# The last image's closing pass cut into three parts in a convolution kernel on one core

## The chip, the core and the metric

The kernel runs on one core of one Trainium2 chip. The metric is the device time of one execution in microseconds, the median of several runs. All engines are written by their short names: PE is TensorE (the matrix unit), DVE is VectorE, ACT is ScalarE, POOL is GpSimd, and SP is SyncE, which here only issues transfers between HBM and the on-chip memory.

## The reference

A batch of four images x of 96 channels and 128 by 128 pixels passes through two blocks. The first is a state-space block (projection, depthwise convolution, four scans, a layer norm over channels, a second projection), added to x. The second one, with which this change deals, is per image:

```python
m, v = mean and variance over channels and pixels
x1, x2 = relu_split_norm(norm(x))          # positive and negative half, each normalised
out0 = 0.5 * (nc1 * x1n + nc2 * x2n) + res_coef * x
k, q, val = conv3x3(x1, aw1), conv3x3(x2, aw2), conv3x3(x1, aw3)
W = softmax(patches(k) @ patches(q).T)      # a 3x3 kernel for every pair of channels
o = conv3x3(val, W)                         # "own": each image has its own weights W
c2 = conv3x3(x2, w_conv2)                   # "second map"
y = w_full[:, 0] @ norm(o) + w_full[:, 1] @ (norm(c2) * x1) + b_full + out0 + x
```

The exact scaling factors do not matter here. What matters: the output of an image needs a product with `norm(o)`, and the statistics of `o` are known only when the last row of its own convolution is done. The product with `norm(c2) * x1` needs the statistics of c2, and those are known as soon as the maps are done, before the own convolution begins. The thresholds (`x > thr`), which give x1 and the residual, need the normalised image alone.

## The kernel before

**Two streams.** The program is written as Python generators that yield a cost. `co_run(left, light, pace)` lets a heavy stream (left) emit its instructions and lets a light one follow in proportion to the yielded costs. A scheduler then lays out each engine's order; each engine runs its own order strictly, and waits on semaphores where data come from elsewhere. For the images b = 1 to 3 left is `attention(img, at)`. The light stream holds the next image's normalisation and split, and then the closing pass of the image before, `imgs[b - 1].close(psr, "right")`. Whatever of the light stream is left when image b begins is emitted ahead of it (`drain(light)`).

**The attention of an image** goes over 11 chunks of 12 rows (the last one of 8) and has two phases:

1. The maps. For each chunk there are four products (`products`, L1470 and L1485): a convolution with 128 outputs and one with 64 for the two halves x1 and x2. Each convolution is done as six products with transformed weights. ACT copies the sums out of PSUM (L1541), and DVE puts them together (`outputs`, L1555 to L1563). Between them PE does the patch products (L1746, L1636). POOL copies the values (L1974) and makes their transformed planes. After the last chunk `taps.weights()` makes the softmax and the transformed weights, which are stacked as `wa`.
2. The own convolution with `wa`, one product per chunk. DVE takes statistics of each chunk (L2034), and SP stores it to `od` in HBM (L2037).

Inputs are loaded by SP two chunks ahead: `ya` (L1879) and `yc` (L1887). `own`, `oc`, the rings of patch rows and the stacks of weights lie in pools of the left side.

**The closing pass** is `attn_output`. It first makes the statistics: of o (`so`, `ro`) by way of `combine` (L186 to L197), of c2 by way of L2170 to L2187. From these come the two 96 by 96 weights `w1` (L2191) and `w2` (L2193) and a constant per channel `lb` (L2197). Then it goes over 16 strips of 8 rows (1024 pixels). For each it loads `o`, `c2` and `xx` (L2203, SP, 384 KB each, one strip ahead, two buffers), makes x1 (ACT L2213, DVE L2214), scales c2 (DVE L2215) and makes the residual e (ACT L2219, DVE L2220 and L2221). For each half of 512 pixels two matmuls add up in one PSUM bank (L2225 with `o`, L2226 with `c2`). DVE adds `lb` and e, and for the images 1 to 3, whose pixels lie in another order, does that in four pieces of 128 (L2237). For image 0 it is one piece (L2228). SP stores the strip (L2239).

The closing passes of the images 0 to 2 run beside the attention of a later image. The last image has none after it:

```python
    drain(light)
    drain(imgs[NB - 1].close(psr, "right"))
```

Of the kernel before, what the change touches and what calls it, by code (L numbers as in the profile page):

```python
# [9 lines left out]
F32 = mybir.dt.float32  # L10
BF16 = mybir.dt.bfloat16
AF = mybir.ActivationFunctionType
ALU = mybir.AluOpType
# [4 lines left out]
C = 96  # L18
# [39 lines left out]
HS = 8  # L58

# [9 lines left out]
def kernel(  # L69
# [1779 lines left out]
    class Attention:  # L1849
# [3 lines left out]
        def __init__(self, ps, p1, p2):  # L1853
            self.ps, self.p1, self.p2 = ps, p1, p2
            self.later = Later()
            chunks = strips_of(AR // 2)
            self.chunks = [(c[0][0], sum(r for _, r in c)) for c in chunks]
            self.todo = [(0, 2, c) for c in self.chunks]
            for b in range(1, NB):
                self.todo += [(b, m, c) for c in self.chunks for m in (0, 1)]  # L1860
                self.todo += [(b, 2, c) for c in self.chunks]
            self.raw, self.cols, self.c = {}, {}, 0
# [62 lines left out]
    def attention(img, at):  # L1925


        ps, p1, p2, later, chunks = at.ps, at.p1, at.p2, at.later, at.chunks
# [5 lines left out]
        if not img.mapped:  # L1934
            taps = PairTaps(ps, later, p1)
# [4 lines left out]
            def value_out(r0, r):  # L1940

                def f():
                    hr = r // 2
                    for i, a in enumerate((0, hr)):

                        def then(pl, a=a):
                            store_planes(nc.sync, img.vp[0:64], r0 + a, hr, pl[0:64])
                            store_planes(nc.sync, img.vp[64:96], r0 + a, hr, pl[96:128])

                        later(planes_of(  # L1950
                            later, p2, own[:, a * PP :], hr, then, AR // 2, bufs=1, p=128
                        ), 3 * i)

                return f

            for s, (r0, r) in enumerate(chunks):
                hr = r // 2
                for m in (0, 1):
# [32 lines left out]
                    if m:  # L1991
                        oc = p2.tile([128, AR // 2 * W], F32, name="oc", bufs=1)
# [31 lines left out]
            ws = product_stack(p1, taps.wt, "wa", nc.scalar)  # L2024
        else:
            ws = product_stack(p1, img.watd, "wa", nc.scalar)
        yield 3.0
        for i, (r0, r) in enumerate(chunks):
            t, fill, load = at.strip()
            oc = own[0:C, : AR * W]  # L2030

            def out(oc=oc, r0=r0, r=r):
# [4 lines left out]
                nc.sync.dma_start(img.od[:, r0 * W : (r0 + r) * W], oc[:, : r * W])  # L2037
# [110 lines left out]

    def attn_output(img, ps, side):
        keep = img.keep  # L2150
        up, low, thr, scale, shift = (keep[n] for n in ("up", "low", "thr", "scale", "shift"))
        ob = out[img.b].rearrange("c h w -> c (h w)")
        with (
# [3 lines left out]
            so, _ = combine(ps, img.ost.rearrange("p c s -> p (c s)"), mean96, "so")  # L2157
            ro = col("ro")
            rsqrt(ro, so[:, 1:2])


            n = NSTRIP
            mva, mvb = (p1.tile([128, 2], F32, name=f"mv_{i}") for i in "ab")
            for mv, st, p, e, k in (
                (mva, img.c2a, 96, 128, 4 * n - 1 if img.mapped else 3 * n - 1),
                (mvb, img.c2b, 0, 64, 2 * n - (not img.mapped)),
                (mvb, img.c2b, 64, 128, 2 * n - 1),
            ):
                v = st[p:e, :k].rearrange("p c s -> p (c s)")
                nc.vector.bn_aggr(mv[p:e], v)  # L2170
            halves = ((mva[96:128], m96[96:128]), (mvb, mrows[img.mapped]))

            def over(n):
                pt = bank(ps)[:, 0:n]
                for i, (mv, mat) in enumerate(halves):
                    nc.tensor.matmul(
                        pt, lhsT=mat, rhs=mv[:, 0:n], start=(i == 0), stop=(i == 1)
                    )
                return pt

            s2 = p1.tile([128, 2], F32, name="s2")
            nc.vector.tensor_copy(s2, over(2))
            for mv, p in ((mva, 96), (mvb, 0)):
                d = mv[p:128, 0:1]
                nc.vector.tensor_sub(d, d, s2[p:128, 0:1])
                nc.vector.tensor_mul(d, d, d)
            nc.vector.tensor_add(s2[:, 1:2], s2[:, 1:2], over(1))  # L2187
            r2 = col("r2")
            rsqrt(r2, s2[0:C, 1:2])
            w1 = p1.tile([C, C], F32, name="w1")  # L2190
            nc.vector.tensor_scalar(w1, wful[:, 0], ro, None, ALU.mult)  # L2191
            w2 = p1.tile([C, C], F32, name="w2")
            nc.vector.tensor_scalar(w2, wful[:, 1], r2, None, ALU.mult)  # L2193
            pt = bank(ps)[:C, 0:1]
            nc.tensor.matmul(pt, lhsT=w1, rhs=so[:, 0:1], start=True, stop=True)
            lb = col("lb")
            nc.vector.tensor_sub(lb, low[:, 1:2], pt)  # L2197

            def loads(t):
                got = []  # L2200
                for name, src in (("o", img.od), ("c2", img.c2d), ("xx", img.xnew)):
# [6 lines left out]
            for t in range(NS):  # L2208
# [4 lines left out]
                nc.scalar.activation(x1, xx, AF.Identity, scale=scale[:, 0:1], bias=shift[:, 0:1])  # L2213
                nc.vector.scalar_tensor_tensor(x1, xx, thr, x1, ALU.is_gt, ALU.mult)  # L2214
# [4 lines left out]
                nc.scalar.activation(e, xx, AF.Identity, scale=up[:, 0:1], bias=up[:, 1:2])  # L2219
                nc.vector.scalar_tensor_tensor(e, xx, thr, e, ALU.is_gt, ALU.mult)  # L2220
                nc.vector.scalar_tensor_tensor(e, xx, low[:, 0:1], e, ALU.mult, ALU.add)  # L2221
                for h in range(2):
# [4 lines left out]
                    if img.mapped:  # L2227
                        nc.vector.scalar_tensor_tensor(x1[:, sl], pf, lb, e[:, sl], ALU.add, ALU.add)  # L2228
                    else:
                        for a in range(0, CH, W):  # L2230
                            px, pe, po = (
                                v[:, a : a + W].rearrange("p (j t) -> p j t", j=TW)
                                if i < 2
                                else v[:, a : a + W].rearrange("p (t j) -> p j t", j=TW)
                                for i, v in enumerate((pf, e[:, sl], x1[:, sl]))
                            )
                            nc.vector.scalar_tensor_tensor(po, px, lb, pe, ALU.add, ALU.add)  # L2237
                    yield 2.6
                nc.sync.dma_start(ob[:, bass.ts(t, SN)], x1)  # L2239

    class Image:


        def __init__(self, b):
# [9 lines left out]
            self.finished = False  # L2254
            self.watd = None if b else dram.tile([C, 3, NP, C], F32, name="watd", bufs=1)
# [114 lines left out]
    for i, rows in enumerate((H // 2, H // 2 + 1)):  # L2370
# [4 lines left out]
    wp = ctx.enter_context(tc.tile_pool(name="wpairs", bufs=1, side="left"))  # L2375
    pairs = []
    at = Attention(
        psl,
        ctx.enter_context(tc.tile_pool(name="d1", bufs=1, side="left")),
        ctx.enter_context(tc.tile_pool(name="d2", bufs=2, side="left")),  # L2380
    )
    at.begin()
    pairs.extend(product_stack(wp, wd, f"wd{i}") for i, wd in enumerate(four))
    for b in range(NB):
        after = []
        if b:
# [3 lines left out]
            if b + 1 < NB:  # L2390
                imgs[b + 1] = Image(b + 1)
                after.append(imgs[b + 1].norm(yms[(b + 1) // 2][(b + 1) % 2], psr, "right"))
                after.append(imgs[b + 1].split(psr, "right", lambda i, second: second))
            after.append(imgs[b - 1].close(psr, "right"))
        light = chain(light, *after)
# [4 lines left out]
    drain(imgs[NB - 1].close(psr, "right"))  # L2400
# [75 lines left out]
```

## Time and profile before

| what | value |
|---|---|
| median of three runs | 6673.67 us (6661.18 to 6675.5) |
| the profiled execution's own time | 6664.87 us |
| its span, first to last instruction | 6663.1 us |
| PE, DVE, ACT, POOL busy | 81%, 73%, 57%, 52% of the span |
| maps of the last image, where no light stream runs beside them | 6060 to 6400 us |
| own convolution of the last image | 6407 to 6513 us |
| closing pass of the last image alone | 6513 to 6663 us |

The busy share of an engine is an average over stages with different limits, so the stages are to be read one by one. The profiled execution took 1.8 us more than its span, and it lies 8.8 us (0.13%) under the median of the runs. Sums are made against the profiled execution; a predicted median then carries the same difference.

### The profile page before, as it was taken

How to read it: one execution, taken by the hardware profiler on the slowest of the kernel's cores; microseconds unless marked ns; L12 is line 12 of the kernel's file. 1: busy time of each engine (PE TensorE's matmuls, PEld its weight loads, DVE VectorE, ACT ScalarE, POOL GpSimd, SP SyncE). 2: the span in 40 equal slices, each digit the busy share in tenths (PEclk: the TensorE clock that was granted, in tenths of full speed). 3: DMA queues.
4: the chain of work that ended last, by engine and by line, in shares of the span. 5: the costliest groups of instructions: out<-in, count | busy, mean ns of one | idle time of the engine just before them, and what ended most of it. 6: DMA issues, size and time to landing. Idle time of an engine off the chain costs nothing. (4 is left out here: it accounts for less than half of the span.)

```text
span 6663.1 us, 76540 instructions
## 1 busy us (share of the span) xinstructions
PE 5393.7 (81%) x23256; PEld 2343.1 (35%) x23256; DVE 4885.0 (73%) x7737; ACT 3810.5 (57%) x4751; POOL 3437.4 (52%) x2683
## 2 busy tenths in 40 slices
PE   5889978988887626989985579877889777878996
PEld 2333323322221103434433243444333454335642
DVE  3247778988997568979756884588865788887557
ACT  1257768777776576767534554565444664535552
POOL 2236658878786436969622363465124574023410
PEclk9999989988997758999997788988879887989987
DMA  7766777866765666765676766556765555865454
GB/s 166 173 156 180 198 212 199 225 180 171 221 186 162 186 175 208 203 194 175 196 189 175 205 167 165 157 148 163 200 182 159 145 159 153 227 164 145 103 149 143
DMA packets 882102, 1176.27 MB, mean 177 GB/s; under 512 B 215230, under 2 KB 740102, under 8 KB 869212
## 3 DMA queue, kind: packets, MB, share of 16 engines
q1 hardware_dynamic: 858076, 1116.43, 61.9%
q0 software_dynamic: 16208, 38.42, 2.1%
q10 hardware_dynamic: 7408, 16.53, 0.8%
q8 instruction: 187, 3.06, 0.2%
q14 instruction: 223, 1.83, 0.1%
HBM read 766.61 MB, written 334.57 MB: 165 GB/s over the span
## 5 line engine op out<-in xcount | busy, mean ns | idle before, releaser
L621 PE MATMUL bank<-y,wp 128*128 128x512 f32 (+3 forms) x3584 | 1315.3, 623 | 84.3 <-DMA y<-y 34.0
L854 POOL TENSOR_TENSOR y<-y,dl 128x1024 f32<-128x1024 f32 x384 | 1051.3, 2738 | 267.8 <-DVE dl L846 237.1
L821 POOL TENSOR_TENSOR dl<-dl,u 128x1024 f32<-128x1024 f32 x384 | 1007.5, 2624 | 228.0 <-ACT dA L797 116.3
L842 DVE TENSOR_TENSOR_SCAN dA<-dA,pBC 128x512 f32<-128x512 f32 x768 | 981.7, 1278 | 30.7
L1470 PE MATMUL two<-ya,wd 128*64 128x192 f32 (+3 forms) x2376 | 590.5, 426 | 189.5 <-ACT odd L1541 106.6
L735 PE MATMUL pBC<-xr,wbc 60*128 60x512 bf16 (+1 forms) x1536 | 457.1, 402 | 333.8 <-DVE dA L842 260.4
L846 DVE TENSOR_TENSOR dl<-dA,pBC 128x512 f32<-128x512 f32 x768 | 528.8, 689 | 268.2 <-PE pBC L735 195.2
L621 PEld LDWEIGHTS bank<-y,wp 128*128 128x128 f32 (+3 forms) x3584 | 458.3, 169 | 753.5 <-issue 655.5
L2096 PE MATMUL bank<-y,wn 128*128 128x384 f32 (+5 forms) x2408 | 675.2, 503 | 42.2 <-DMA y<-x2d 19.3
L1904 ACT COPY yb<-ya 64x768 f32<-64x768 f32 (+1 forms) x660 | 538.4, 816 | 170.3 <-PE two L1470 121.7
L664 ACT ACTIVATE dl<-pd,dtb 128x512 f32<-128x512 f32 x768 | 486.3, 684 | 185.3 <-PE pd L735 176.9
L1470 PE MATMUL two<-yb,wd 128*64 128x192 f32 (+3 forms) x2376 | 565.2, 410 | 0.0
L825 DVE TENSOR_TENSOR pBC<-dl,pBC 128x512 f32<-128x512 f32 x768 | 527.5, 687 | 9.7 <-POOL dl L821 8.8
L2096 PEld LDWEIGHTS bank<-y,wn 128*128 128x128 f32 (+3 forms) x2408 | 307.4, 167 | 336.8 <-issue 168.7
L1974 POOL COPY own<-ring 32x512 f32<-32x512 f32 (+1 forms) x198 | 219.4, 1144 | 393.7 <-DVE ring L1563 327.0
L797 ACT ACTIVATE dA<-dl,negA 128x1024 f32<-128x1024 f32 x384 | 420.4, 1142 | 2.3
L1470 PEld LDWEIGHTS two<-ya,wd 128*64 128x64 f32 (+1 forms) x2376 | 267.1, 172 | 394.8 <-ACT odd L1541 115.3
L735 PEld LDWEIGHTS <-wbc 60*128 60x128 bf16 (+1 forms) x1536 | 103.5, 96 | 767.9 <-issue 754.2
L664 ACT ACT_TABLE_LOAD x245 | 314.3, 1283 | 99.3 <-PE pd L735 92.0
L1470 PEld LDWEIGHTS two<-yb,wd 128*64 128x64 f32 (+1 forms) x2376 | 293.5, 172 | 151.5 <-issue 43.2
L1470 PE MATMUL two<-ya,wa 128*96 128x384 f32 (+1 forms) x528 | 228.7, 516 | 132.7 <-DMA wa<-watd 86.3
L1001 PE MATMUL bank<-y,outws 96*96 96x512 f32 x512 | 296.7, 710 | 3.5 <-DVE r L1014 2.3
(309 smaller groups left out, 9675.7 us busy)
## 6 DMA issues: line engine op xcount, KB each, us to landing
u<-zb SPq DMA_DIRECT2D x192, 1024.0 KB
yms<-y SPq DMA_DIRECT2D x96, 512.0 KB
y<-yms SPq DMA_DIRECT2D x64, 768.0 KB
xn<-xnew SPq DMA_DIRECT2D x128, 384.0 KB
ya<-vp SPq DMA_DIRECT2D x120, 336.0 KB
y<-y SPq DMA_DIRECT2D x128, 258.2 KB
zb<-z SPq DMA_DIRECT2D x64, 512.0 KB
ya<-x1p SPq DMA_DIRECT2D x90, 336.0 KB
```

Source lines behind the costliest of these rows:

```text
L621: nc.tensor.matmul(blocks(pz[p:e]), lhsT=ws[k][:, d, c : c + e - p], rhs=window(ys[k], at, d, n), start=(i == 0), stop=(i == len(terms) - 1),)
L664: nc.scalar.activation(dst, src, AF.Softplus, bias=bias)
L735: nc.tensor.matmul(p, lhsT=w[rows], rhs=xr[rows, at : at + CH], start=True, stop=True)
L797: nc.scalar.activation(live[m]["dA"], live[m]["dl"], AF.Exp, scale=negA[:, g % 3, k : k + 1])
L821: nc.gpsimd.tensor_mul(t, t, u_view(n))
L825: nc.vector.tensor_mul(p, live[n]["dl"][:, bass.ts(half, CH)], p)
L842: nc.vector.tensor_tensor_scan(h, h, p, init, ALU.mult, ALU.add)
L846: nc.vector.tensor_mul(live[n]["dl"][:, sl], live[n]["dA"][:, sl], live[n]["C", half])
L854: nc.gpsimd.tensor_add(v, v, t.rearrange("p (a b) -> p a b", b=W))
L1470: nc.tensor.matmul(of(to[p:e], r), lhsT=w[:, i, c : c + e - p], rhs=tiles(t[k][PAIR[i]][:, SLOT[i]], o, r), start=(k == 0), stop=False,)
L1904: nc.scalar.copy(yb[k][64 * h - 64 : 64 * h, :, :n], ya[k][0:64, :, h * TN : h * TN + n])
L2096: nc.tensor.matmul(pc[p:e, :n].rearrange("p (h w) -> p h w", w=W), lhsT=w[:, c : c + e - p], rhs=v[:, :, 0:W], start=(i == 0), stop=(i == ...
```

## The change

The closing passes of the images 0 to 2 keep their place. In all of them the constant `lb` goes into the first product: the tile `o` gets a 97th row of ones (a memset by POOL for every tile), and `w1` gets a 97th row with the constant. The last DVE operation is then a plain addition, one of 512 pixels for either order of pixels. The last image's pass becomes a class with three parts. `before` and `beside` are put behind the light stream of the last attention. `after` runs when the attention is over.

- `before` makes x1 and e of all strips and stores them to HBM (`x1s`, `es`).
- `beside` waits until the maps are made. It then makes the statistics and the weight of c2, loads c2, x1 and e strip by strip, multiplies, and adds the product and e into a tile `kept` that holds the whole image on chip (64 KB per partition). That tile takes the place of what only the maps needed; those tiles have moved to a pool of their own (`pm`), which is closed then.
- `after` loads `o` of the first 12 strips (six buffers), makes `w1`, and for each strip does one product per half, one addition of 1024 pixels to `kept`, and the store. The last 32 rows of o are not stored to `od` at all: the own convolution writes them into a tile with its row of ones. The strips from these rows come first.

The core of the diff:

```diff
@@ attention
+            img.maps_made()
...
             oc = own[0:C, : AR * W]
+            here = img.last and r0 >= H - OWN
+            if here:
+                oc = img.last.own[0:C, (r0 - H + OWN) * W :]
...
-                nc.sync.dma_start(img.od[:, r0 * W : (r0 + r) * W], oc[:, : r * W])
+                if not here:
+                    nc.sync.dma_start(img.od[:, r0 * W : (r0 + r) * W], oc[:, : r * W])
@@ own_weights (new; c2_weights holds the rest of the old head)
+        w1 = pool.tile([128, C], F32, name="w1")
+        nc.vector.tensor_scalar(w1[0:C], wful[:, 0], ro, None, ALU.mult)
+        nso = col("nso")
+        nc.vector.tensor_scalar(nso, so[:, 0:1], -1.0, None, ALU.mult)
+        pt = bank(ps)[C : C + 1, 0:C]
+        nc.tensor.matmul(pt, lhsT=img.keep["low"][:, 1:2], rhs=ident, start=True, stop=False)
+        nc.tensor.matmul(pt, lhsT=nso, rhs=w1[0:C], start=False, stop=True)
+        nc.vector.tensor_copy(w1[C : C + 1], pt)
+        return w1[0 : C + 1]
+
+    def with_ones(pool, name, bufs=None):
+        y = pool.tile([128, SN], F32, name=name, tag=name, bufs=bufs)
+        nc.gpsimd.memset(y[C : C + 1], 1.0)
+        return y[0 : C + 1]
@@ attn_output
-                        for a in range(0, CH, W):
...
-                            nc.vector.scalar_tensor_tensor(po, px, lb, pe, ALU.add, ALU.add)
+                        nc.vector.tensor_add(plain(x1[:, sl]), pixels(pf), pixels(e[:, sl]))
@@ class LastOutput (new)
+        def before(self):
...
+                for t in range(NS):
...
+                    first_half(img, xx, x1)
+                    yield 2.0
+                    residual(img, xx, e)
+                    yield 2.6
+                    for d, y in ((self.x1d, x1), (self.ed, e)):
+                        nc.sync.dma_start(d[:, bass.ts(t, SN)], y)
+        def beside(self):
+            while self.kept is None:
+                yield None
...
+                s2, w2 = c2_weights(img, self.ps, p1)
...
+                    nc.vector.scalar_tensor_tensor(
+                        c2, c2, s2[0:C, 0:1], x1, ALU.subtract, ALU.mult
+                    )
+                    for h in range(2):
...
+                        nc.tensor.matmul(pf, lhsT=w2, rhs=c2[:, sl], start=True, stop=True)
+                        nc.vector.tensor_add(
+                            plain(self.kept[:, t, sl]), pixels(pf), pixels(e[:, sl])
+                        )
+                        yield 2.2
+        def after(self, pairs):
...
+                for t in range(here):
+                    o = with_ones(p3, "o")
+                    nc.sync.dma_start(o[0:C], img.od[:, bass.ts(t, SN)])
+                    loaded.append(o)
+                w1 = own_weights(img, self.ps, p1)
+                for t in (*range(here, NS), *range(here)):
...
+                    for h in range(2):
+                        nc.tensor.matmul(
+                            pf[:, h], lhsT=w1, rhs=o[:, bass.ts(h, CH)], start=True, stop=True
+                        )
+                    to = self.kept[:, t]
+                    nc.vector.tensor_add(
+                        plain(to), pixels(pf.rearrange("p h w -> p (h w)")), plain(to)
+                    )
+                    nc.sync.dma_start(ob[:, bass.ts(t, SN)], to)
@@ the program's end
             after.append(imgs[b - 1].close(psr, "right"))
+            if b + 1 == NB:
+                last = imgs[b].last = LastOutput(imgs[b], psr, "right")
+                imgs[b].maps_made = lambda: maps_made(last)
+                after += [last.before(), last.beside()]
...
-    drain(imgs[NB - 1].close(psr, "right"))
+    at.later.flush()
+    drain(last.after(psl))
```

`first_half` and `residual` are the old lines L2213, L2214 and L2219 to L2221 under a name; `here` in `after` is 12.

## The prediction

> **What bounds the kernel now.** I read the busy slices of the page first, then the stages one by one (busy time in chosen windows), then the groups of the last stage and its timeline. The table of stages carries most of the argument. Its columns are the stretch, its length, the busy time of PE, weight loads, DVE, ACT and POOL (with counts), the granted PE clock, the busy share of the DMA engines, and GB/s.
>
> ```profile
> 5628.00:5812.00 184.00, 163.19 (x489) 66.71 (x490) 167.53 (x293) 97.54 (x111) 0.00 (x0) 0.95 0.87 229
> 5842.00:6049.00 207.00, 167.06 (x718) 77.89 (x716) 175.76 (x313) 82.84 (x95) 60.47 (x67) 0.89 0.66 174
> 6111.00:6315.00 204.00, 193.34 (x1441) 126.02 (x1440) 121.28 (x235) 106.22 (x141) 91.07 (x130) 0.98 0.42 107
> 6420.00:6510.00 90.00, 90.00 (x339) 40.02 (x338) 65.81 (x114) 57.45 (x72) 0.00 (x0) 1.00 0.74 189
> 6513.00:6663.00 150.00, 95.65 (x142) 31.01 (x142) 115.69 (x218) 36.86 (x32) 0.00 (x0) 0.69 0.52 154
> ```
>
> In order: image 2's own convolution with image 1's close beside it; the last image's maps with image 2's close beside them; the same maps alone; the last own convolution alone; the last close alone. Alone, PE is full (193 of 204 us, 90 of 90). With a close beside, DVE is at 85 to 91%, and PE has gaps. In the last close nothing is full: it goes strip by strip.
>
> ```profile
> L2226 PE MATMUL bank<-c,w 96*96 96x512 f32 x64 | 52.0, 932 | 26.2 <-DVE c L2215 26.2
> L2237 DVE SCALAR_TENSOR_TENSOR x<-bank,lb,e 96x128 f32<-96x128 f32 x128 | 38.0, 424 | 26.2 <-PE bank L2226 25.7
> ```
>
> These groups of the last stage show the two engines waiting for each other by turns. Its start and its end, in the timeline (start, length):
>
> ```profile
> 6512.46 0.38 PE L1485 MATMUL two<-ya,wa 32*96 32x256 f32 x2
> ...
> 6527.51 2.00 PE L2225 MATMUL bank<-o,w 96*96 96x512 f32 x2
> ...
> 6531.26 1.22 DVE L2237 SCALAR_TENSOR_TENSOR x<-bank,lb,e 96x128 f32<-96x128 f32 x4 [3.04 <-PE bank L2226]
> ...
> 6657.60 1.22 DVE L2237 SCALAR_TENSOR_TENSOR x<-bank,lb,e 96x128 f32<-96x128 f32 x4 [1.18 <-PE bank L2226]
> ```
>
> The last convolution ends at 6512.9. The first product starts 14.6 us later, the strips take 131.3 us (8.2 each), and 4.3 us after the last DVE operation the span ends: 150.2 us in all. The rates of the other stages are read from the DVE operation that ends each product of the attention:
>
> ```profile
> 5842.26 0.34 DVE L1555 TENSOR_TENSOR wide<-odd,two 128x192 f32<-128x192 f32 x1
> 6049.04 0.55 DVE L1555 TENSOR_TENSOR wide<-odd,two 128x384 f32<-128x384 f32 x1 [7.29 <-ACT odd L1541]
> 6111.20 0.56 DVE L1555 TENSOR_TENSOR wide<-odd,two 128x384 f32<-128x384 f32 x1 [5.63 <-ACT odd L1541]
> 6315.43 0.56 DVE L1555 TENSOR_TENSOR wide<-odd,two 128x384 f32<-128x384 f32 x1 [5.63 <-ACT odd L1541]
> 6420.31 0.55 DVE L1555 TENSOR_TENSOR wide<-odd,two 96x384 f32<-96x384 f32 x1 [16.96 <-ACT odd L1541]
> 6430.03 0.55 DVE L1555 TENSOR_TENSOR wide<-odd,two 96x384 f32<-96x384 f32 x1 [2.47 <-ACT odd L1541]
> ```
>
> Between the third and the fourth lie 20 products: 10.2 us each alone. Between the first and the second lie 9: 23 us each with a close beside. A chunk of the own convolution takes 9.72 us alone.
>
> **What the Trainium skill says.** "VectorE: DVE Perf Modes", in its section on the TRN2 errata, gives an fp32 tensor_tensor as (N+151)/0.96 ns: 691 for N = 512 and 1224 for N = 1024. The trace agrees (677 median for the 512 addition from PSUM of L1014, 962 for 768 columns of L1561). "TensorE: Matmul & The Clock Gate", Part 1, says that PE falls to half its clock when idle and comes back after about 3.4 us of work. The last close shows both rates: products 1.71 us apart after waits, 0.86 us when busy. "DMA: Bandwidth & Descriptors", under "Issuing engines are not separate DMA queues", says that all issuers share the same 16 engines; so I price loads by the DMA share of the stage and not by queue.
>
> **The change, part by part.** The order of the changed program, as built, tells which operations stand in which product.
>
> *The last part, alone at the end.* The 14.6 us up to the first product keep their chain (statistics, root, w1, one more small product and a copy). They lose the c2 statistics and two L2215 of 1.27 us between, so I take 13. Then come 32 products of 512 columns: four at 1.71 and 28 at 0.86 us are 31 us, PE's end at +44. DVE needs 16 additions at 1.22, 20 us, hidden beside PE. DMA: the first six loads of `o` are issued behind the last `ya`, with the convolution still running. The other six wait for the products of the strips whose buffers they take, and in SP's order 12 of the 16 stores stand behind them. The sixth buffer is free after 10 strips, at about 13 + 6.8 + 16 × 0.86 = +34. From there 12 × 0.39 MB at about 290 GB/s (154 at a share of 0.52 in the last close) take 16 us: +50, plus the 4 us of landing. **+54 instead of +150: −96 us** (−102 to −86).
>
> *The part beside the own convolution.* PE gets 32 products of 0.86 us. In the built order the first strips' operations (nine on DVE, about 2.5 strips) stand in the hole in which PE waits for the new weights before the first chunk (DVE idle 16.96 in the line above). That leaves 13.5 strips over 11 chunks, 1.23 each. Per chunk: PE 9.72 + 1.23 × 1.72 = 11.8 us; DVE 7.1 + 1.23 × (1.20 + 2 × 0.68) = 10.2; DMA 0.74 × 9.72 = 7.2 us of full use, plus 1.23 × 1.18 MB at 290 GB/s = 5.0, 12.2 in all. Three resources lie near each other, so I add 0.7 for waits: 12.9 us. **11 × 3.2 = +35** (PE's floor +23; with a sixth lost +58). What waits: the products stand in PE's order inside the chunk, so a late c2 holds back the convolution; the loads stand in SP's order ahead of the `ya` of two chunks later.
>
> *The part beside the maps.* No PE work. Each strip brings DVE three operations (means 1.37, 1.35 and 1.32 us while a close runs beside), ACT two of 1.24, and SP a load and two stores of 384 KB. In the built order two strips stand in each product, over 8.3 products, right behind image 2's close. DVE: 0.59 × 10.2 = 6.0 us of its own plus 8.1, 14.1 us, against 10.2 alone: this stretch turns from PE-bound to DVE-bound. 8.3 × 3.9 is 32 us with a full DVE, 42 with the gaps it had beside the close; **I take +37** (26 to 45). ACT (10 us) and DMA (0.42 × 10.2 + 8 = 12.3) stay under it. The stores wait for DVE in SP's order; behind them stand `ya` loads, which have two chunks in hand.
>
> *The addition in one piece.* Images 1 and 2: 4 × 0.305 (L2237 x4 in 1.22) become 0.68 per half, −1.08 us per strip, −17 on DVE for each close. Image 2's runs at a DVE of 85%: **−15** (−20 to −8). Image 1's runs at DVE 91% and DMA 0.87, so DMA is next late: **−12** (−17 to −4). Image 0 keeps its count: nothing.
>
> *The rows of ones.* A 97th row costs PE nothing that I can see: L2225 with 96 rows takes 594 ns for 512 columns, L1470 with 128 rows 517 for 384. Memsets: 48 in the closes, one large one, 12 in the last part. Nearest rows: POOL memsets of 129 and 1292 columns, 213 and 1172 ns, so about 0.95 us for 1024. POOL is idle beside image 1's close and has a third busy beside image 2's, so the work hides. But each waits for its buffer, that is for PE two strips back, and behind it stand L1974 and the planes, whose buffers DVE then needs. Bounds 0 to +10; **I take +3**. The store of the last 32 rows that falls away (1.57 MB, 5 us of DMA) is inside the waits above.
>
> **Sum:** −96 + 35 + 37 − 15 − 12 + 3 = −48. The profiled execution of 6664.9 becomes 6617; the median of 6673.7, 8.8 above it, becomes **6626**.
>
> **Rivals.**
> - *All covers at their floor.* The tail −102, the convolution +23, the maps +26, the closes −37: −90, a median of 6584. For it: in the alone stages PE ran without a gap. Against: no co-run stage of before did, PE had 81 to 89% there.
> - *All given back.* Maps +45, convolution +58, closes −12, tail −88, memsets +5: +8, no change to be measured, 6682. For it: image 2's close cost (23 − 10.2) × 9 = 115 us although its own work alone takes some 131; hardly a tenth was hidden. Against: the moved parts are lighter on PE, and what remains at the end is short by itself.
> - *Slower: the strip's chain stands in PE's way in the own convolution.* SP holds each strip's three loads until a buffer (two deep) is free, PE stops inside the chunk at the product that lacks c2, and nothing overlaps. A strip then costs its chain: load 4.0 us, DVE 1.2, two products 1.7, addition 0.7: 7.6 us, 13.5 of them 103 us instead of 35. Net +20, a median of 6694. It decides from a strip cost of about 7.1 us. For it: L2226 waited 26.2 us for L2215 in the last close. Against: image 2's own convolution, with four loads and a store per strip, moved 229 GB/s beside the products, so transfers do overlap.
> - *It does not do what it says:* the loads of `beside` could be held until the maps' pool is free. The built order puts its first products ahead of the first chunk, so I give that no chance of its own.
>
> **Chances.** My sum with its own range (−75 to −20) 0.68; covers at their floor 0.14; given back 0.09; slower by the chain 0.09. A difference of 0.2% (13 us) is about what a measurement of this kernel can tell from no change. From the first two cases nearly all is faster by more: 0.81. Within 0.2%: 0.08 from the third and 0.02 from the edge of the first: 0.10. Slower: 0.09. The range goes from the floor case (6584) to just beyond no change (6677).
>
> **What would show it.** Right: from the last convolution product to the end of the span about 54 us, the last stores close behind each other; a chunk of the own convolution 12 to 14 us with PE above 85%; the products beside the first part about 14 to 15 us apart with DVE above 90%; the addition of 512 columns near 0.68 us. Wrong: a chunk above 17 us, PE waiting on L2336's result (the changed kernel's scaling of c2); stores at the end spread over more than 70 us; POOL memsets as the releaser of L1974's or DVE's waits.

## The result, and the profile after

| | before | after |
|---|---|---|
| median of six runs beside each other | 6674.81 us (6661.18 to 6686.55) | 6639.86 us (6631.00 to 6649.60) |
| ratio, with its 95% interval | | 0.9947 [0.9932, 0.9961] |
| the profiled execution, and its span | 6664.87, 6663.1 us | 6633.80, 6631.9 us |

The median fell by 35 us; 48 were predicted. The profiled executions are 31 us apart. Lines of the kernel after are those of before plus one up to about L1990 (L1555 is now L1556); the closing passes have new ones.

Busy time by stage in the kernel after, columns as before (stretch, length, PE, weight loads, DVE, ACT, POOL, PE clock, DMA share, GB/s). In order: image 2's own convolution with image 1's close; the maps with image 2's close; the maps with the first part; the maps alone; the own convolution with the second part; the end alone.

```profile
5609.00:5788.00 179.00, 158.49 (x487) 64.75 (x487) 162.67 (x206) 96.03 (x111) 13.25 (x14) 0.97 0.86 231
5830.00:5976.00 146.00, 127.47 (x622) 61.73 (x623) 134.46 (x155) 65.90 (x74) 61.20 (x65) 0.94 0.69 185
5976.00:6168.00 192.00, 144.17 (x769) 79.38 (x768) 153.13 (x202) 100.88 (x115) 66.36 (x68) 0.84 0.65 185
6209.00:6330.00 121.00, 114.54 (x870) 75.21 (x870) 73.38 (x143) 63.93 (x85) 54.56 (x78) 1.00 0.49 128
6430.00:6580.00 150.00, 136.23 (x434) 57.24 (x432) 113.85 (x163) 60.92 (x77) 5.41 (x6) 0.94 0.88 228
6583.00:6632.00 49.00, 32.64 (x72) 12.29 (x72) 25.24 (x33) 0.20 (x1) 5.68 (x6) 0.79 0.58 177
```

The close of 150 us is now 49 (last line). But the third line has PE at 75% and DVE at 80%: neither full. In the fifth PE is at 91%, DVE only at 76%, DMA at 0.88. The groups of its ten chunks from 6437.6 to 6581.0 answer to L2226 and L2237 of before:

```profile
L2342 PE MATMUL bank<-c,w 96*96 96x512 f32 x54 | 27.9, 630 | 11.5 <-DVE c L2336 11.5
L2343 DVE TENSOR_TENSOR e<-bank,e 96x512 f32<-96x512 f32 x27 | 27.4, 1036 | 17.1 <-PE bank L2342 17.1
```

One addition of 512 columns takes 1036 ns; the prediction had 0.68 us. The end, in the timeline (start, length):

```profile
6580.23 0.68 PE L1486 MATMUL two<-ya,wa 32*96 32x256 f32 x4
...
6591.09 30.79 PE L2366 MATMUL two<-o,w 97*96 97x512 f32 x64 [0.45 <-DVE w L2204]
...
6621.92 1.22 DVE L2370 TENSOR_TENSOR e<-two,e 96x1024 f32<-96x1024 f32 x1 [0.50 <-PE two L2366]
```

From the end of the last convolution product (6580.9) it is 10.2 us to the first product, 30.8 us of PE without a stop, 1.2 us of DVE, and 8.8 us until the last store has landed and the span ends at 6631.9: 51 us. SP issues the last six loads of `o` up to 6612 and only then the 12 stores that stand behind them. The transfers are nearly full in that stretch (columns as in the table of stages):

```profile
6612.00:6628.00 16.00, 9.88 (x24) 3.43 (x22) 8.16 (x7) 0.00 (x0) 0.64 (x1) 0.90 0.97 307
```

The pace of the two covered parts is read from the same DVE operation as before, again in the timeline:

```profile
6030.82 0.54 DVE L1556 TENSOR_TENSOR wide<-odd,two 128x384 f32<-128x384 f32 x1
...
6156.74 0.34 DVE L1556 TENSOR_TENSOR wide<-odd,two 128x192 f32<-128x192 f32 x1
...
6437.62 0.56 DVE L1556 TENSOR_TENSOR wide<-odd,two 96x384 f32<-96x384 f32 x1
...
6581.04 0.42 DVE L1556 TENSOR_TENSOR wide<-odd,two 96x256 f32<-96x256 f32 x1 [6.26 <-PE two L1486]
```

Between the first two lie seven products of the maps: 18.0 us each beside the first part, against 10.3 for the same seven before. Between the last two lie ten chunks: 14.3 us each beside the second part, against 9.4 for the same ten before. The busy times of these stretches, the seven products before and after, then the ten chunks before and after:

```profile
6068.88:6141.03 72.15, 65.94 (x536) 44.29 (x535) 48.47 (x85) 43.03 (x56) 37.08 (x51) 1.00 0.42 109
6030.82:6156.74 125.92, 88.61 (x526) 52.03 (x524) 100.63 (x127) 67.77 (x77) 48.91 (x52) 0.77 0.66 192
6420.31:6514.14 93.83, 92.53 (x355) 41.48 (x353) 69.85 (x120) 58.36 (x73) 0.00 (x0) 1.00 0.72 185
6437.62:6581.04 143.42, 129.53 (x411) 54.17 (x409) 109.47 (x161) 56.80 (x72) 5.41 (x6) 0.94 0.87 225
```

The seven products became 54 us longer although the first part gives PE no work: PE stands idle for 31 us more, and the same products keep it busy for 23 us more, at a granted clock of 0.77 instead of 1.00. The ten chunks became 50 us longer: 28 us are the new products (L2342), 9 us more go to the convolution's own products at a clock of 0.94 instead of 1.00, and 13 us more PE is idle. Waits and a lower clock come together here; which brings the other isn't shown.

**Where the time went.** The same 176 operations of L1556 stand in every kernel, so the distance between the time of one of them and its time before can be followed. A step in that distance is what a stage gained (minus) or lost. In us, rounded, one profiled execution each; `ones_only`, `split_only` and `no_before` are experiments told below:

| stretch, by the times of before | after | ones_only | split_only | no_before |
|---|---|---|---|---|
| start to 4732 | −10 | +18 | −3 | +3 |
| image 0's close, start of image 3's normalisation (to 5090) | −15 | −9 | 0 | −19 |
| to the start of image 2's own convolution (5576) | +4 | +10 | +5 | +4 |
| that convolution, with image 1's close (to 5809) | 0 | +4 | +1 | +4 |
| maps with image 2's close, first part (to 6337) | +36 | −18 | +51 | −18 |
| last own convolution (to 6514) | +53 | 0 | +48 | +73 |
| the end | −98 | 0 | −98 | −99 |
| sum: distance of the spans | −31 | +6 | +3 | −52 |

The first row holds nothing that changed; it shows how far single executions drift apart, by −15 to +19 us over all kernels told below, so the medians decide on totals. The profiled execution of `ones_only` was the slowest of its seven, that of `split_only` the fastest of its 22. Image 2's close gives −18 where it stands without the first part (`ones_only`, `no_before`), so the first part costs 36 + 18 = 54 us. The cut itself is then −98 + 54 + 53 = +9, and in `split_only` −98 + 51 + 48, about 0: **no gain at all.** What the kernel gained came from the closes of the other images; the medians of `ones_only` and `split_only` say the same below.

### The profile page after: what moved, and what is told of

The parts are those of the page before. It is cut to its first block, busy times and chain, and to the rows that moved or that the text cites. A ratio compares the mean times of both kernels' runs of the same rounds, so it can differ in the third digit from the quotient of the medians.

```text
span 6631.9 us, 76453 instructions
## 1 busy us (share of the span) xinstructions
PE 5374.8 (81%) x23264; PEld 2337.9 (35%) x23264; DVE 4907.7 (74%) x7469; ACT 3803.6 (57%) x4751; POOL 3506.9 (53%) x2744
## 5 line engine op out<-in xcount | busy, mean ns | idle before, releaser
L2209 POOL MEMSET o<- 1x1024 f32 x60 | 56.3, 946 | 560.3 <-PE bank L2264 225.3
```

## The experiments

All were timed beside the kernel before. Differences of ratios are turned into us with 6673.

| kernel | median, runs | ratio to before [95%] | us |
|---|---|---|---|
| ones_only | 6637.62, 7 | 0.9956 [0.9940, 0.9972] | −29 |
| split_only | 6685.83, 22 | 1.0019 [1.0009, 1.0029] | +13 |
| spread | 6632.73, 5 | 0.9937 [0.9925, 0.9949] | −42 |
| xx_ahead | 6646.01, 10 | 0.9958 [0.9944, 0.9971] | −28 |
| turned_add | 6638.07, 5 | 0.9949 [0.9936, 0.9962] | −34 |
| no_before | 6611.26, 6 | 0.9917 [0.9898, 0.9935] | −55 |
| no_before_turned | 6614.54, 6 | 0.9918 [0.9903, 0.9934] | −55 |
| no_e_load | 6638.08, 6 | 0.9949 [0.9934, 0.9964] | −34 |
| ones_four | 6653.42, 10 | 0.9971 [0.9959, 0.9983] | −19 |
| no_constant | 6636.81, 5 | 0.9948 [0.9932, 0.9964] | −35 |
| half_before | 6627.49, 5 | 0.9932 [0.9917, 0.9947] | −45 |
| no_store | 6641.48, 6 | 0.9949 [0.9931, 0.9968] | −34 |

Two theories of the total are to be told apart: **Theory A**, the covered parts were priced too low, so the tail's gain is handed back and the closes bring all of the gain; **Theory B**, that of the prediction, the cut brings 24 us (−96 + 35 + 37) and the closes bring 24.

### The halves of the change

`ones_only` keeps the rewritten closes and puts the last image's close back at the end in one piece:

```diff
-                last = imgs[b].last = LastOutput(imgs[b], psr, "right")
...
-                after += [last.before(), last.beside()]
...
-    drain(last.after(psl))
+    drain(imgs[NB - 1].close(psr, "right"))
```

> The row of ones and the single addition stay in all four closing passes; the last image's pass is one piece at the end again, as before the change. If the prediction's size for the closes was right, it is 24 us faster than before (15 and 12 from the additions, 3 lost to memsets). If the slower addition seen in the trace (1.03 us for 512 columns where 0.68 was counted, against 1.22 for the four pieces) is the whole of it, it gains some 0.4 us a strip, at most 15 us over the images 1 and 2 and the tail, and image 1's closing pass gains nothing. If the 20 us by which the changed kernel was ahead before image 2's own convolution come from this part of the change, the same 20 us show here at the same place; if they were chance, they do not.

`split_only` is the reverse: the three parts, with `attn_output` for the images 0 to 2 as it was (`lb` as an operand of L2318, four pieces, no row of ones).

> The closing passes of the images 0 to 2 are those of the kernel before (constant by lb, four additions of 128, no memsets); only the last image's pass is cut in three parts. Theory A, from the run with the ones alone: the cut itself gives nothing, what the end loses (98 us) comes back beside the maps (54) and beside the own convolution (53); this kernel then lies within 12 us of the kernel before, and well above the changed one. Theory B, that of the prediction: the cut gives 24 us (-96, +35, +37) and the closes 24; then it lies 24 us or more under the kernel before. The gain of 17 us at the start of image 3's normalisation, which all kernels with the ones showed at 4960 to 5046 us, should be missing here if it comes from the rewritten closing pass of image 0.

The rewritten closes alone bring 29 us. The cut alone makes the kernel 13 us slower, with an interval that leaves out 1. Theory B falls. The two effects don't add up exactly (−29 + 13 = −16, the first uncertain by 11 us, the second by 7, against −35 with an interval of −45 to −26); in single executions the cut's own terms in `split_only` and in the kernel after differ by 5 us at most (table above).

### What in the closes gave the gain

`ones_four` is `ones_only` with the addition of the images 1 to 3 in four pieces again:

```diff
-                        nc.vector.tensor_add(plain(x1[:, sl]), pixels(pf), pixels(e[:, sl]))
+                        for a in range(0, CH, W):
...
+                            nc.vector.tensor_add(po, px, pe)
```

> The closes as in ones_only (row of ones, no three parts), but the addition of images 1 to 3 again in four pieces of 128 columns. ones_only was 35 us under the kernel before. If the one-piece addition brings that gain (DVE 0.37 us less per strip and fewer instructions in the closes that run at a DVE of 85 to 91%), most of it is lost here: about 6660 us, and the tail and image 2's close as before. If the gain comes with the row of ones itself (the constant no longer read as an operand, the closing pass in another order), it stays: within 6 us of ones_only, 6632 to 6644.

`no_constant` is `ones_only` without memsets and 97th row; it leaves the constant out of the output:

```diff
-                o = with_ones(p3, "o")
+                o = p3.tile([C, SN], F32, name="o")
...
-            w1 = own_weights(img, ps, p1)
+            w1 = own_weights(img, ps, p1)[0:C]
```

> ones_only without the row of ones: the closes leave out the constant in all four images, so there are no memsets on POOL and the products contract 96 rows. The addition stays in one piece. If the 48 memsets and the 97th row are hidden, the time is that of ones_only within 4 us (about 6638). If the memsets stand in the way of POOL's planes, it is some 10 us under it. If the gain of ones_only needs the row, it goes to about 6670.

Without row and memsets the time is 6636.81 against 6637.62: the row of ones costs nothing that can be measured. Its memset is this line of the groups of the page of the kernel after:

```profile
L2209 POOL MEMSET o<- 1x1024 f32 x60 | 56.3, 946 | 560.3 <-PE bank L2264 225.3
```

With four pieces 10 us of the 29 go by the ratios, 16 by the medians, though the two intervals overlap by 9 us. Against `no_constant`, which was timed beside the same executions of the kernel before, it is 15 us by the ratios and the intervals hardly touch. So neither expectation was right: part of the gain is most likely the single piece, and 19 us stay without it. In the aligned traces the single piece acts on image 2's close alone (+13 us with four pieces, −18 with one); image 1's close is no slower with four (−3 against +4). The pieces read in order and write at a stride, the single addition the other way round; that isn't what helps, since with the single addition turned (`no_before_turned`, below) image 2's close gains 19 us too. The pieces' DVE time doesn't explain it. These are the groups of DVE while image 2's close runs, in `ones_four`, in `ones_only` and in the kernel before:

```profile
L2276 DVE TENSOR_TENSOR x<-bank,e 96x128 f32<-96x128 f32 x128 | 33.0, 396 | 18.2 <-PE bank L2265 18.2
```

```profile
L2269 DVE TENSOR_TENSOR x<-bank,e 96x512 f32<-96x512 f32 x31 | 31.2, 1032 | 2.1 <-PE bank L2265 1.8
```

```profile
L2237 DVE SCALAR_TENSOR_TENSOR x<-bank,lb,e 96x128 f32<-96x128 f32 x128 | 37.4, 428 | 3.6 <-PE bank L2226 3.6
```

Per half that is 33.0/32 = 1.03, 31.2/31 = 1.01 and 37.4/32 = 1.17 us. Four pieces or one, the plain addition keeps DVE busy equally long; the sum with the operand `lb` takes about 0.15 us longer, 5 us for a close. `ones_four`'s DVE waits 16 us more for PE there, and its granted clock in that stretch was 0.82 against 0.96, which may be the wait's cause or its consequence. Why one piece is faster stays open, and so does the gain of 8 to 19 us between 4732 and 5090, which every kernel with the rewritten closes has and `split_only` has not. About 2 us of it are the additions of image 0's close, 32 of which take 680 ns each where the sum with `lb` took 742.

### The first part: its load, its queue, its loads and its stores

`spread` and `xx_ahead` change the yields and the buffers of `before`, `no_store` leaves out its stores (the second part then loads xnew in place of x1 and e):

```diff
 # spread
-                    yield 2.0
+                    yield 5.2
...
-                    yield 2.6
+                    yield 6.8
 # xx_ahead
-                ahead = load(0)
+                ahead = [load(t) for t in range(4)]
 # no_store
-                    for d, y in ((self.x1d, x1), (self.ed, e)):
-                        nc.sync.dma_start(d[:, bass.ts(t, SN)], y)
```

> As the changed kernel, but the first part yields 12 per strip in place of 4.6, so that its 16 strips stand in about twenty products of the maps instead of eight. If that stretch costs time because too much DVE work stands in each product (6.0 + 8.1 us against PE's 10.2), one strip less per product fits (6.0 + 3.2) and the cost of the stretch falls from some 60 us to under 20: a median 35 to 45 us under the changed kernel. If it costs because the strips' stores and loads on SP and the ACT operations behind them make PE wait at each strip, each strip still costs its 3 to 4 us and the gain is under 10 us.

> As the changed kernel, but the first part loads x four strips ahead instead of one. If ACT's waits for that load (10.4 us in the stretch) and the copies for PE behind them make the stretch long, its cost falls by 20 us or more. If DVE's load sets it, it stays within 5 us of the changed kernel.

> The changed kernel without the 32 stores of x1 and e (12.6 MB left out); the part beside the own convolution loads xnew in their place, as many bytes in as many loads, so its output is not the reference's. If the loads of ya and xx held up behind the stores in SP's queue make the maps stretch lose 54 us, the products beside the first part come back to 14 us or less and the time falls by 15 us or more, to 6625. If DVE's load or ACT's own order makes the loss, it stays within 5 us of 6640.

In the aligned traces the first part costs 54 us in the kernel after, 44 with `no_store`, about 42 with `xx_ahead` and 28 with `spread`. In the medians only `spread` is under the kernel after, by 7 us, and the two intervals overlap; `xx_ahead` is 6 us above it. So neither of the gains that were held possible, 35 us and more by spreading and 20 us and more by loading ahead, was there. What PE and ACT waited for in the kernel after, from 5976 to 6168 (us in total, times, longest):

```profile
PEld two L1471 <- ACT yb L1905: 24.6, 5, 11.4
...
PE two L1471 <- ACT yb L1905: 21.3, 4, 10.8
DVE x L2215 <- ACT x L2214: 14.5, 5, 4.6
...
ACT x L2214 <- DMA xx<-xnew: 10.4, 5, 5.4
```

PE stands up to 11 us before a copy of ACT (`yb`), which stands in ACT's order behind L2214, which waits for `xx`; SP issues that load behind the stores. With `no_store` no wait of PE for `yb` is among the waits of the same window. The median is the same: 6641.48 against 6639.86. The seven products of above, in `no_store`:

```profile
6054.67:6169.96 115.29, 83.20 (x518) 52.58 (x515) 98.75 (x126) 71.32 (x81) 52.20 (x58) 0.75 0.55 142
```

They take 16.5 us each instead of 18.0, still far from 10.3. DVE is at 86%, and PE is idle for 32 us of 115, now before other results of ACT and DVE; its clock is 0.75. So the chain SP, ACT, PE was there, but it is worth 10 us of the 54 in the trace and nothing that the medians show. DVE's load, which comes in bursts, is what is left as a reading; it is not shown by itself, and PE's lower clock is part of the price whatever brings it. Spreading the same work thin halved its price in the trace, yet the rest stayed, though DVE has 40% to spare where the maps run alone.

### No first part, or half of one

`no_before` drops the first part. The second loads c2 and xx, and makes x1 and e itself:

```diff
-                after += [last.before(), last.beside()]
+                after += [last.beside()]
...
-                    for name, src in (("c2", img.c2d), ("x1", self.x1d), ("e", self.ed)):
+                    for name, src in (("c2", img.c2d), ("xx", img.xnew)):
...
+                    first_half(img, xx, x1)
+                    residual(img, xx, e)
```

> The first part is dropped: beside the own convolution x itself is loaded, and x1 and e are made there; no stores and loads of x1 and e at all (18.9 MB of transfers less beside the maps, 6.3 MB less beside the convolution). The maps then cost nothing more than in the run with the ones alone (54 us less than the changed kernel). Beside the convolution DVE gets 1.23 x (4 x 1.2 + 2 x 1.03) = 8.4 us a chunk on top of 7.1. If DVE sets the pace there, a chunk takes about 16.5 us instead of 14.3 (24 us more in all): a median near 6610. If ACT and SP in their order add waits as beside the maps, a chunk takes 18 us and more (45 us), and the gain shrinks to 10 us.

`half_before` makes x1 and e of the strips 8 to 15 beside the maps, thinly, and those of 0 to 7 beside the own convolution:

```diff
-                for t in range(NS):
+                for t in range(NS // 2, NS):
...
-                    yield 2.0
+                    yield 10.4
...
-                    yield 2.6
+                    yield 13.6
```

> The three parts, but x1 and e of strips 8 to 15 alone are made beside the maps, thinly spread (weights 10.4 and 13.6 instead of 2.0 and 2.6), and those of strips 0 to 7 beside the own convolution from xnew. no_before (all made beside the own convolution) was 6611. If DVE sets the pace of the own convolution there (147.6 of 160 us busy), 8 strips of 4 us of DVE work less give back some 25 us, and the maps, where DVE has 40% to spare, cost at most half of what spread lost, about 14: 6600 or less. If it is the queues in their order and not DVE's load, the gain and the loss cancel: 6605 to 6617.

`no_before` is the best of all, 6611.26 (−55 us, −26 more than `ones_only`). With half the first part it is 6627, above it by 16 (by 10 in the ratios, whose intervals overlap), where a DVE bound in the own convolution had led to expect 11 less. The windows of `no_before` (maps after image 2's close; own convolution) and of `half_before` (own convolution, strips made there, then strips loaded):

```profile
5976.00:6168.00 192.00, 175.27 (x1142) 106.37 (x1139) 133.76 (x215) 94.79 (x121) 87.68 (x107) 0.96 0.55 142
...
6400.00:6560.00 160.00, 136.16 (x406) 56.16 (x404) 147.60 (x193) 84.96 (x96) 5.41 (x6) 0.87 0.64 167
```

```profile
6430.00:6500.00 70.00, 64.19 (x189) 25.10 (x190) 66.66 (x86) 38.18 (x44) 0.00 (x0) 0.90 0.72 190
6500.00:6575.00 75.00, 68.80 (x236) 28.90 (x234) 61.73 (x92) 30.24 (x40) 5.41 (x6) 1.00 0.85 223
```

In `no_before` DVE is the fullest engine in the own convolution, at 92%, and that stretch costs 73 us instead of 53. But it loads two tensors for each strip instead of three, and the maps lose nothing: the cut is −99 + 73 = −26 us, as much as lies between the medians of `ones_only` and `no_before`. In `half_before` each half has another fullest engine: DVE at 95% first, PE at 92% with DMA at 0.85 then. It loses 52 us there, as much as the kernel after, and 22 in the maps on top: −24 in its trace. So leaving out the first part helps, and half of it is no better than none; whether half is worse isn't settled.

### What sets the pace beside the own convolution

`turned_add` lets the additions of 512 columns walk in the order in which PSUM and e lie, and write at a stride (`no_before_turned` is `no_before` with the same edit):

```diff
+                        rows = "p (h j t) -> p h j t"
...
-                            plain(self.kept[:, t, sl]), pixels(pf), pixels(e[:, sl])
+                            self.kept[:, t, sl].rearrange("p (h t j) -> p h j t", j=TW, t=TN),
+                            pf.rearrange(rows, j=TW, t=TN),
+                            e[:, sl].rearrange(rows, j=TW, t=TN),
```

> As the changed kernel, but the addition walks in the order of the pixels: reads of the PSUM bank and of e are contiguous, the write is strided by four. If the stride of 32 elements in e is what makes the addition 1.03 us, it falls to about 0.68 us (0.35 us less, 64 times in the closes of the images 1 and 2 and 32 times beside the own convolution). If DVE sets the pace beside the own convolution, its chunks fall by 0.9 us each, 10 us in all, and the closes gain up to 10 us each; if DMA sets it (its share was 0.88), nothing changes there and the median stays within 5 us of the changed kernel.

> As the kernel without the first part, and the addition walks in the order of the pixels. With DVE as the bound there, its 1.23 x 2 x 0.35 = 0.9 us a chunk less show: 10 us under it. If the addition is no faster in this order, or DVE is not the bound, the two are the same within 4 us.

Neither moved (6638.07; 6614.54), but they tell nothing of the bound, since the edit didn't do what it was made for. The group of the addition in `turned_add`:

```profile
L2349 DVE TENSOR_TENSOR e<-bank,e 96x512 f32<-96x512 f32 x32 | 33.8, 1097 | 27.0 <-PE bank L2347 26.9
```

1097 ns, slower than the 1036 of before the edit.

`no_e_load` loads e for the first strip only and uses it in all, 5.9 MB of loads less:

```diff
-                    for name, src in (("c2", img.c2d), ("x1", self.x1d), ("e", self.ed)):
+                    for name, src in (("c2", img.c2d), ("x1", self.x1d)):
```

> As the changed kernel, but beside the own convolution e of the first strip is loaded once and used for all strips, so the output is not that of the reference; this leaves out 5.9 MB of loads and no other work. If DMA sets the pace there (share 0.88), a chunk falls from 14.3 us by 1.23 x 0.39 MB at 260 GB/s, 1.8 us, some 18 us in all, and PE becomes the bound at about 12 us. If PE or DVE or their turns set it, the chunk stays within 0.5 us.

The median is that of the kernel after (6638.08), the stretch in the trace 13 us shorter (40 instead of 53). Five other kernels with three loads for each strip lose 48 to 50 us there, so 8 to 13 us are e's loads. Its ten chunks:

```profile
6436.55:6567.22 130.67, 120.31 (x410) 50.55 (x408) 108.97 (x160) 57.20 (x72) 5.41 (x6) 0.99 0.81 207
```

DMA has gone from 0.87 to 0.81, the clock from 0.94 to 0.99, and PE stays at 92%. So DMA is part of the price in the trace, though the medians don't show it; 40 of 53 us are something else. PE's floor was 23 us in the prediction; the new products took 28 in the kernel after. What PE waits for there is nearly one thing: of 13.9 us of idle time, 11.5 are for the scaling of c2 (L2336). No run here takes that wait away.

## Why the prediction was right, and where its sum was wrong

The direction of the total is right and its size 13 us off (−35 for −48). But the cut, which was to bring half of it, brought nothing, and that the total came out near is in good part luck: the closes brought about what was forecast for them (−24), and by other terms than those in the sum. Term by term:

| term | predicted | measured in the trace |
|---|---|---|
| the end alone | −96 | −98 |
| part beside the own convolution | +35 | +53 |
| part beside the maps | +37 | +54 |
| image 2's close | −15 | −18 |
| image 1's close | −12 | 0 |
| memsets, row of ones | +3 | 0 (medians) |
| image 0's close and what follows it | 0 | −15 (−8 to −19) |

- **The end.** 51 us for 54, and by the way that was forecast. PE's products ran on without a wait (30.79 us for 31). DMA was the last to be late, for six loads of `o` and the stores behind them: the stores could start 31 us after the last convolution product (34 predicted), 12 of them moved at 307 GB/s (290 predicted), and the span ended 8.8 us after the last addition.
- **Beside the own convolution** the term was 12.9 us a chunk; it took 14.3, and the stretch up to its first chunk lost time too. The step that failed is PE's price, 11.8 us a chunk: PE was busy for 13.0, as long as the whole chunk was to take. The sum priced PE at the pace that it has alone; the new product took 1.03 us instead of 0.86, and the convolution's own products took 9 us more over the ten chunks, at a lower clock. The idle time of PE was 1.4 us a chunk, and the wait was the one that was named, a late c2. DMA's 12.2 us became 12.5. DVE's 1.03 us for the addition is another mis-sized number (10.9 us of DVE a chunk for 10.2); whether DVE was the bound wasn't shown, since the faster addition that was to test it was not faster.
- **Beside the maps** the term was 14.1 us of DVE for each product, and it took 18.0 at a DVE of 80%. The DVE work itself was right (100.6 us for seven products, 14.4 each). The failed step is the sentence that a stage with a DVE work of 14.1 runs at 14.1, and with it "no PE work": PE's own products became 3 us longer each, at a clock of 0.77. Image 2's close, in the first profile, had said otherwise: 23 us a product at a DVE of 85%. I took +37 from a range of 26 to 45, whose upper part held those gaps (42); even that was too low.
- **The addition in one piece.** I took 0.68 us from the Trainium skill, "VectorE: DVE Perf Modes", on the TRN2 errata: (512+151)/0.96 = 691 ns, an estimate. The measurement decides against it for these strides. The additions in the kernel after (min, median and max in ns; L2267 is image 0, where nothing is strided, L2269 the images 1 and 2, L2343 and L2370 the last image):

```profile
L2269 DVE TENSOR_TENSOR x<-bank,e x64: 1016/1034/1057, 5619.0 to 6015.3; 96x512 f32<-96x512 f32 x64
L2267 DVE TENSOR_TENSOR x<-bank,e x32: 657/680/689, 4770.9 to 4885.8; 96x512 f32<-96x512 f32 x32
L2343 DVE TENSOR_TENSOR e<-bank,e x32: 1009/1036/1060, 6426.0 to 6567.7; 96x512 f32<-96x512 f32 x32
L2370 DVE TENSOR_TENSOR e<-two,e x16: 1220/1220/1221, 6594.8 to 6621.9; 96x1024 f32<-96x1024 f32 x16
```

  The saving was 1.17 − 1.01 per half, not 0.54. So the −15 for image 2 came out by another way than reckoned. The same products of the maps from the start of its close to its end, before and in `ones_only`:

```profile
5824.05:6132.68 308.63, 257.92 (x1360) 134.98 (x1356) 248.93 (x442) 136.98 (x163) 101.12 (x121) 0.92 0.59 157
5845.70:6138.69 292.99, 255.04 (x1386) 134.27 (x1380) 245.07 (x341) 137.13 (x165) 125.57 (x141) 0.96 0.62 165
```

  DVE's busy time fell by 4 us and not by 17; 12 of the 16 us are DVE's idle time. Why it shrank stays open. Nothing was left for image 1, whose stretch moves 231 GB/s at a DMA share of 0.86, as before (229, 0.87). That "DMA is next late" there was in the text; whether DMA or the missing saving on DVE kept the gain away, no run separates.
- **The memsets** hide, at 946 ns as priced (0.95 us).
- **The rival "all given back"** was right on the cut and wrong on the closes: it had +15 for the cut, −12 for the closes and +8 for the total; the cut by itself is 0 to +9 in the traces and +13 in the medians. I gave it 0.09, and its mechanism (hardly a tenth of a close's cost is hidden) deserved more. The rival of the chain inside the convolution did not come at its size: PE did wait for c2, but a strip cost 53/13.5 = 3.9 us, not 7.1.

## What to carry to other kernels

Work moved under a stage can cost more than the busy time that it adds to the fullest engine: here 16 strips under two stages cost 107 us where 98 were saved, at a DVE of 80% and 76%, and the engine that was full before was slowed in its own work. Look at a stretch of the same profile where a similar stream already runs beside, and price by the busy share that is reached there, not by a full engine: with DVE at 85%, as beside image 2's close before, the 14.1 us of a product become 16.6, nearer to the 18.0 measured. And do half the change alone before you believe in a total: the cut, for which the change was made, brought nothing, the rewritten closes brought all of the gain, and leaving out the most elaborate part (an early pass through HBM) brought 29 us more by the medians, 20 by the ratios.

## What the runs showed that I had not expected

- In the table of additions above, an fp32 addition of 512 columns takes 680 ns with all operands in order and 1034 with e read from SBUF at a stride of 32 elements. With the write at a stride of 4 elements instead it takes 1076 (median of the 64 in `turned_add`). A stride in the PSUM operand alone costs nothing: L2370, 1024 columns in 1220 ns, reads it so, where the formula of the same page of the Trainium skill, "VectorE: DVE Perf Modes", gives an estimate of 1224.
- A wait that is prominent in the trace can be taken away with little gain: PE's 21 us before `yb` are gone in `no_store`, other waits stand in their place, the stage is 10 us shorter in the trace, and the median is the same.
- PE's own products take longer beside another stream, even one without PE work: the same seven products of the maps kept PE busy for 89 us instead of 66, at a granted clock of 0.77 instead of 1.00.
